# Turned B, x and sums behind later projections, a five-term log1p series, and products tied to the newest projection, in a Mamba-2 block on one core

## The chip, the cores and the metric

The kernel runs on 1 core of one Trainium2 chip (trn2). The metric is the device time of the whole kernel in microseconds (us); the number compared is the median over several runs. A core has five engines that work side by side: TensorE (PE, matmuls), VectorE (DVE), ScalarE (ACT), GpSimd (POOL) and SyncE (SP), which here issues the DMA transfers. Data lies in SBUF; matmuls write to PSUM.

## The reference

The input x has 4 rows of 512 tokens and 512 features. `c` gives, through a small product, six vectors for each row (shift, scale and gate of two branches).

```python
h = _layernorm(x) * (1 + ca) + sa
x = x + ga * attn(h)
h = _layernorm(x) * (1 + cb) + sb
x = x + gb * ffn(h)

# attn: Mamba-2 with chunks of 128 tokens
xBCzA = einsum('bld,ed->ble', h, in_proj_w)      # 2048 conv channels, 1024 z, 64 heads' A
xBC = silu(causal_conv4(xBCzA[..., :2048]) + conv_bias)   # x 1024, B 8 x 64, C 8 x 64
dt = softplus(A_log)                             # one per token and head
y = ssd_chunk_scan(x, -dt, B, C, 128) + D * x / dt
attn = einsum('bld,ed->ble', y * silu(z + z_bias), out_proj_w)
# ffn: a 512 x 512 product with weights binarized to sign * mean |w|
```

The scan has, for each chunk and head (64 heads of 16 features, 8 heads to a group), a product C·B of 128 x 128, times exp of differences of running sums of dt under a causal mask, times x; a state for each head that is carried from chunk to chunk; and C times that state.

## The kernel before, in words

**Tiling.** The tokens are cut into 8 halves h of 256 tokens, two to a row, and each half into 2 chunks c of 128. For each chunk the 8 groups go in 4 pairs gp; a (h, c, gp) is a unit, so there are 64 units, 8 in a half. One step handles one unit.

**The front of a half** turns tokens into the operands of its units. `load_x` and `f_norm` load and normalise. `f_hT` (L334) turns x with TensorE (tile phT) and writes hT with four ACT instructions (L346). `f_dt` (L352) multiplies hT with the A columns (pa, L367), and then runs a long chain, mostly on DVE, for softplus: u = exp(-|a|), then log1p(u) as the odd series 2 (w + w³/3 + …) in w = u / (u + 2). Its coefficients are SERIES (L36), one DVE scalar_tensor_tensor (STT) for each after the first (L379). After that come running sums of dt (L384), exps of them (L390 on), and the DMAs of sums, exps and D/dt to scratch in DRAM. `f_B`, `f_C`, `f_x` each make a pair of conv projections: `conv_pair` (L436) takes a PSUM tile (pp_), has `proj` (L431) issue four matmuls into it (L433), and reads it with one ACT instruction (L446) and three DVE STTs (L450); then tanh (L454) and a product (L455) for silu. `f_z` does the same without conv (uz, L512; thz, L516). `f_turned_sums` (L414) turns the sums with TensorE (pn) and copies them to st by ACT (L426); `f_Bt` (L476) turns B to tokens (pt_bt); `f_xt` (L485) turns x (pt_xt, L463), copies it with ACT into a padded tile xpad (L489), loads rr = D/dt on SP's queue (L498), and has POOL multiply (xs, L503).

**A unit** is made in three stages. `stage0` loads the running sums into a decay tile for each of the two groups r of the pair (`load_sums`, L537 and L538, two DMAs each on SP's queue). There are four such decay buffers, so a load waits until an earlier unit has done with the buffer. `stage1` multiplies the causal mask with C·B (gm, L619), runs `exps` (L545: 8 ACT instructions for each group, 16 a unit; bias from st) and multiplies both on DVE (L623). `stage2` makes py from decay and xpad, 16 small matmuls for each r, adds the contribution of the state and the skip term (L669 to L673), and updates the state from pst (L685). `burst` (L594) makes the products gy: C with the state for the current unit, C·B for a unit ahead. The tails of a chunk, `tail1` to `tail3`, are the output projection (po, L722), the second norm, its turn (ph, L740; h, L742) and the FFN product (pf, L758).

**Order of the work.** A scheduler of the framework orders the instructions within each engine from priorities and dependences, in the order in which the Python code issues them; engines wait for each other by semaphores. On top of it lie three means. Lists of steps, FIRST (half 0), SECOND (half 1) and FRONT (the later halves, L770), say in which step of the previous half's units a part of h's front is issued. `behind` (L764) puts a part after the last projection that was issued for that half (`tc.issue_after(H[h]["last"])`). `glued` (L208) issues the first of a group of small products (L211), and then the rest right after it with high priority (L214), so that the group stays together; it may take an instruction to come after. All PSUM tiles with the tag "mm" (projections, turns, pa, po, pf, pst, and so on) share five buffers, so each of them waits until the tile five before it has been read.

TensorE runs matmuls in four shapes of tiling: projections, turns, po and pf use all 128 rows and columns; gy has 64 rows, pa and pst 64 columns, py 32 columns.

Of the kernel before, what the change touches and what calls it, by code (L numbers as in the profile page):

```python
# [32 lines left out]

SERIES = [1.0 / k for k in range(17, 1, -2)]  # L36


@with_exitstack
def adaln_mamba_block(  # L40
# [18 lines left out]
    def bc(ap, n):  # L59

        return ap.unsqueeze(2).to_broadcast([ap.shape[0], ap.shape[1], n])
# [146 lines left out]
    def glued(products, after=None):  # L208

        with tc.issue_after(after) if after else nullcontext():  # L210
            first = products[0]()  # L211
        with tc.issue_after(first.ins), tc.high_priority(offset=1000):
            for product in products[1:]:
                product()  # L214
# [89 lines left out]
    H = [dict(B={}, C={}, xt={}, xs={}, bt={}, z={}) for _ in range(NHALF)]  # L304
# [47 lines left out]
    def f_dt(h):  # L352
# [23 lines left out]
        nc.vector.tensor_mul(q, u, u)  # L376
        nc.vector.tensor_scalar(dt, q, SERIES[0], None, ALU.mult)
        for cf in SERIES[1:]:
            nc.vector.scalar_tensor_tensor(dt, dt, cf, q, ALU.add, ALU.mult)  # L379
# [51 lines left out]
    def proj(pm, h, col, lo):  # L431
        for k in range(NK):
            last = mm(pm, win[:, k, col : col + P], H[h]["hT"][:, k, lo:], start=(k == 0), stop=(k == NK - 1))  # L433
        return last.ins

    def conv_pair(h, t0, name, dst=None):  # L436

        u = wk.tile([P, 2, T], F32, tag="u", name=f"u_{name}_{h}", bufs=4)
        for j in range(2):
            t = t0 + j
            pm = ps.tile([P, KS - 1 + T], F32, tag="mm", name=f"pp_{name}{j}_{h}")
            H[h]["last"] = proj(pm, h, t * P, 0)
            nc.scalar.activation(  # L446
                u[:, j, :], pm[:, KS - 1 :], AF.Identity, bias=cb[:, t : t + 1], scale=cw[:, t, KS - 1 : KS]
            )
            for k in range(KS - 1):
                nc.vector.scalar_tensor_tensor(  # L450
                    u[:, j, :], pm[:, k : k + T], cw[:, t, k : k + 1], u[:, j, :], ALU.mult, ALU.add
                )
        th = wk.tile([P, 2, T], F32, tag="th", name=f"th_{name}_{h}")
        nc.scalar.activation(th, u, AF.Tanh)  # L454
        nc.vector.scalar_tensor_tensor(u if dst is None else dst, th, 1.0, u, ALU.add, ALU.mult)  # L455
        return u
# [49 lines left out]
    def f_z(h, j):  # L506
        pm = ps.tile([P, 2, T], F32, tag="mm", name=f"pp_z{j}_{h}")
        for q in range(2):
            H[h]["last"] = proj(pm[:, q, :], h, NCONV + (2 * j + q) * P, KS - 1)
        u = wk.tile([P, 2, T], F32, tag="u", name=f"uz_{h}_{j}", bufs=4)  # L510
        for q in range(2):
            nc.scalar.activation(  # L512
                u[:, q, :], pm[:, q, :], AF.Identity, bias=zb[:, 2 * j + q : 2 * j + q + 1], scale=0.5
            )
        th = wk.tile([P, 2, T], F32, tag="th", name=f"thz_{h}_{j}")
        nc.scalar.activation(th, u, AF.Tanh)  # L516
        z = wk.tile([P, 2, T], F32, tag="z", name=f"z_{h}_{j}", bufs=6)
        nc.vector.scalar_tensor_tensor(z, th, 1.0, u, ALU.add, ALU.mult)
        H[h]["z"][j] = z
# [64 lines left out]
    def by_rows(gy, slot, h, c, gp, stationary):  # L584

        return [
            partial(
                mm, gy[:, r, slot, :], stationary[part],
                H[h]["C"][gp // 2][part, gp % 2, c * CH : (c + 1) * CH], start=True, stop=True,
            )  # L590
            for r, part in enumerate((slice(0, NS), slice(NS, P)))
        ]

    def burst(old, new):  # L594

        gy = ps.tile([P, 2, 4, CH], F32, tag="gy", bufs=1, name="gy_" + "_".join(map(str, old or new)))
        products = []
        if old is not None:
            h, c, gp = old
            k = (h % HPB) * 2 + c  # L600
            if k > 0:
                products += by_rows(gy, 1, h, c, gp, states[h // HPB, k][:, gp, :])
                G[old, 1] = gy
        if new is not None:
            h, c, gp = new
            products += by_rows(gy, 0, h, c, gp, H[h]["B"][gp // 2][:, gp % 2, c * CH : (c + 1) * CH])
            G[new, 0] = gy
        glued(products)

    def stage1(h, c, gp):  # L610

# [16 lines left out]
    def stage2(h, c, gp):  # L628

        n = f"{h}_{c}_{gp}"
        k = (h % HPB) * 2 + c
        b = h // HPB
        ets, e = U1.pop((h, c, gp))
        hd0 = c * NH + gp * HPP
        xp = H[h]["xt"][gp][:, c, :]
        xg = xp.rearrange("p (j q e) -> p j q e", q=4, e=HD)[:, :, 0:4:3, :]

        def by_head(v):

            return v.rearrange("p (j q) -> p j q", q=2).unsqueeze(3).to_broadcast([P, HPG, 2, HD])

        py = ps.tile([P, 2, CH], F32, tag="y", bufs=1, name=f"py_{n}")

        for r in range(2):
            glued([
                partial(
                    mm, py[32 * j : 32 * j + 32, r, :],  # L650
                    xp[:, r * 2 * P + 32 * (2 * j + q) : r * 2 * P + 32 * (2 * j + q) + 32],
                    ets[r][:, 2 * j + q, :], start=(q == 0), stop=(q == 1),
                )
                for q in range(2) for j in range(HPG // 2)
            ], H[1]["last"] if (h, c) == (0, 1) else None)

        cs = slice(c * CH, (c + 1) * CH)
        zg = H[h]["z"][gp][:, :, cs]
        xs = H[h]["xs"][gp][:, :, cs]
        t = wk.tile([P, 2, CH], F32, tag="gm", name=f"yt_{n}", bufs=3)  # L660

        ew = nc.vector if h == NHALF - 1 and c == 1 and gp >= NP // 2 else nc.gpsimd
        if k > 0:
            nc.vector.tensor_mul(t, G.pop(((h, c, gp), 1))[:, :, 1, :], e)
            if ew is nc.vector:
                ew.tensor_add(t, t, xs)
                ew.tensor_add(t, py, t)
            else:
                nc.vector.tensor_add(t, py, t)  # L669
                ew.tensor_add(t, t, xs)  # L670
        else:
            nc.vector.tensor_add(t, py, xs)  # L672
        ew.tensor_mul(zg, t, zg)  # L673

        if k < HPB * 2 - 1:
            if gp == 0:
                states[b, k + 1] = wk.tile([P, NP, P], F32, tag="S", name=f"S_{b}_{k + 1}")
            new = states[b, k + 1][:, gp, :]
            xd = wk.tile([P, HPG, 2, HD], F32, tag="xd", name=f"xd_{n}")
            nc.gpsimd.tensor_tensor(xd, xg, by_head(H[h]["ed"][:, hd0 : hd0 + HPP]), ALU.mult)  # L680
            xd2 = xd.rearrange("p j q e -> p (j q e)")
            pst = ps.tile([P, P], F32, tag="mm", name=f"pst_{n}")
            bt = H[h]["bt"][gp // 2][:, c, gp % 2, :]
            for r in range(2):
                mm(pst[r * NS : (r + 1) * NS, :], bt[:, r * NS : (r + 1) * NS], xd2[:, r * P : (r + 1) * P],  # L685
                   start=True, stop=True)
            if k == 0:
                nc.vector.tensor_copy(new, pst)
            else:
                nc.gpsimd.tensor_tensor(  # L690
                    new.rearrange("p (h e) -> p h e", e=HD),
                    states[b, k][:, gp, :].rearrange("p (h e) -> p h e", e=HD),
                    bc(H[h]["dec"][:, c * NP + gp, :], HD), ALU.mult,
                )
                nc.vector.tensor_add(new, new, pst)
# [68 lines left out]
    def behind(h, f, *args):  # L764
# [4 lines left out]

    FRONT = [  # L770
        (1, load_x, ()), (2, f_norm, ()), (3, f_hT, ()), (3, f_dt, ()),
        (4, f_B, (0,)), (4, f_C, (0,)), (5, f_x, (0,)), (5, f_x, (1,)), (5, behind, (f_turned_sums,)), (5, behind, (f_Bt, 0)),
        (6, f_B, (1,)), (6, behind, (f_xt, 0)), (6, f_C, (1,)), (6, behind, (f_xt, 1)),
        (7, f_x, (2,)), (7, behind, (f_Bt, 1)), (7, f_x, (3,)),
        (8, f_z, (0,)), (8, behind, (f_xt, 2)), (8, f_z, (1,)), (8, behind, (f_xt, 3)),
        (9, f_z, (2,)), (10, f_z, (3,)),
    ]

    FIRST = [
# [7 lines left out]

    SECOND = [
        (0, load_x, ()), (1, f_norm, ()), (2, f_hT, ()), (2, f_dt, ()), (2, f_B, (0,)), (3, f_C, (0,)), (3, f_x, (0,)),
        (4, f_x, (1,)), (4, behind, (f_turned_sums,)), (4, behind, (f_Bt, 0)),  # L790
        (5, f_B, (1,)), (5, behind, (f_xt, 0)),
    ]
    SECOND += FRONT[FRONT.index((6, f_C, (1,))) :]
    NU = 2 * NP
# [28 lines left out]
    h = NHALF - 1  # L823
# [65 lines left out]
```

## Time and profile before

| what | us |
|---|---|
| median of three runs | 749.24 (748.86 to 753.6) |
| the profiled execution | 747.6 |
| span in its profile, first to last instruction | 745.9 |
| PE busy | 711.2 (5196 matmuls) |
| weight loads busy | 503.2 |
| DVE busy | 602.6 (1218 instructions) |
| ACT busy | 523.7 (1507) |
| POOL busy | 260.4 (313) |

The profile is of one execution, so its 747.6 stands beside the median of 749.24; the 1.7 between the execution and its span lie before the first and after the last instruction. The mean clock that TensorE was granted is 0.991 of full speed. A view of waits lists which engine sat idle before which work, and what released it; a timeline gives each instruction or run of equal instructions with its start, its duration and, in brackets, the idle time ahead of it. "PE pp_x L433" is TensorE working on tile pp_x at line 433. The work of the halves repeats: the stretches from 184 to 271, 271 to 361, 361 to 447.5, 447.5 to 536.5 and 536.5 to 623 us each hold one half, with PE busy 85.75 of 87.0, 87.29 of 90.0, 85.25 of 86.5, 87.27 of 89.0 and 85.25 of 86.5.

### The profile page before, as it was taken

What the parts mean: (1) busy time and instruction counts of PE and PEld (TensorE: products, weight loads), DVE (VectorE), ACT (ScalarE), POOL (GpSimd) and SP (SyncE); (2) the same over time, 40 slices, a digit from 0 to 9 for tenths busy, and PEclk for the clock granted to TensorE, in tenths of its full rate; (3) what the DMA queues carried; (4) which work ended last, traced back from release to release, by engine and by line L of the source; (5) the groups of instructions that cost most, each with busy time, mean ns of one, the idle gap of its engine ahead of it and who ended that gap; (6) DMA issues with size and microseconds to landing.
All of it is one profiled execution on the core that took longest, in us unless ns stands there. A gap on an engine that the chain in (4) does not pass through costs nothing.

```text
span 745.9 us, 15107 instructions
## 1 busy us (share of the span) xinstructions
PE 711.2 (95%) x5196; PEld 503.2 (67%) x5196; DVE 602.6 (81%) x1218; ACT 523.7 (70%) x1507; POOL 260.4 (35%) x313
## 2 busy tenths in 40 slices
PE   6999979899999999999999999999999999999997
PEld 3787647566677666686667666876667866677654
DVE  3968889866999579986899769996699867997795
ACT  2476668648796596775877777764969658798941
POOL 4021325334242433353224243533324232343452
PEclk9999989899999999999999999999999999999999
DMA  8991865435654266434634246543544436458610
GB/s 280 317 289 39 237 164 121 113 86 138 125 146 125 63 158 140 106 101 99 158 101 119 75 108 165 149 110 69 139 125 121 129 79 175 104 152 167 143 58 28
DMA packets 119068, 99.25 MB, mean 133 GB/s; under 512 B 73984, under 2 KB 97152, under 8 KB 118992
## 3 DMA queue, kind: packets, MB, share of 16 engines
q1 hardware_dynamic: 117808, 96.39, 50.6%
q0 software_dynamic: 896, 1.38, 0.6%
q8 instruction: 41, 0.67, 0.4%
q10 hardware_dynamic: 288, 0.52, 0.2%
q14 instruction: 35, 0.29, 0.1%
HBM read 92.47 MB, written 5.79 MB: 132 GB/s over the span
## 4 chain that ended last, share of the span: by engine, by line
PE 77%; ACT 14%; DVE 5%; issue 2%; DMA 2%; ACTq 0%; POOL 0%; SPq 0%; DVEq 0%
PE pp_x L433 16%; PE po L722 15%; PE pp_z L433 12%; ACT decay L545 10%; PE pp_B L433 7%; PE pp_C L433 7%; PE pf L758 4%; PE py L211 3%; PE py L214 3%; PE gy L211 2%; PE pt_xt L463 2%; PE pst L685 2%; PE pa L367 1%; DMA decay<-sums_d 1%; ACT h L742 1%
## 5 line engine op out<-in xcount | busy, mean ns | idle before, releaser
L545 ACT ACTIVATE decay<-decay,st 128x128 f32<-128x128 f32 x960 | 293.0, 395 | 4.0 <-DMA decay<-sums_d 3.7
L623 DVE SCALAR_TENSOR_TENSOR decay<-decay,gm 128x1024 f32<-128x1024 f32 x120 | 156.8, 1308 | 25.1 <-ACT decay L545 24.1
L433 PE MATMUL pp_x<-hT,win 128*128 128x259 f32 x512 | 122.5, 394 | 5.8 <-ACT decay L545 5.8
L433 PE MATMUL pp_z<-hT,win 128*128 128x256 f32 x512 | 118.1, 383 | 0.0
L433 PEld LDWEIGHTS pp_x<-hT,win 128*128 128x128 f32 x512 | 98.0, 195 | 24.1 <-ACT decay L545 6.0
L722 PE MATMUL po<-wout,z 128*128 128x512 f32 x256 | 113.9, 595 | 0.0
L433 PEld LDWEIGHTS pp_z<-hT,win 128*128 128x128 f32 x512 | 94.3, 189 | 16.1 <-issue 3.3
L680 POOL TENSOR_TENSOR xd<-xpad,st 128x256 f32<-128x256 f32 x48 | 37.6, 784 | 188.3 <-PE pst L685 143.0
L450 DVE SCALAR_TENSOR_TENSOR u_x<-pp_x,cw,u_x 128x256 f32<-128x256 f32 x192 | 82.9, 473 | 1.4 <-ACT u_x L446 0.5
L722 PEld LDWEIGHTS po<-wout,z 128*128 128x128 f32 x256 | 47.4, 190 | 52.6 <-issue 51.7
L512 ACT ACTIVATE uz<-pp_z,zb 128x256 f32<-128x256 f32 x64 | 26.8, 468 | 62.3 <-PE pp_z L433 62.3
L670 POOL TENSOR_TENSOR yt<-yt,xs 128x256 f32<-128x256 f32 x46 | 41.1, 893 | 84.4 <-DVE yt L669 84.4
L214 PE MATMUL py<-decay,xpad 128*32 128x128 f32 x1680 | 67.4, 276 | 0.0
L673 POOL TENSOR_TENSOR z<-yt,z 128x256 f32<-128x256 f32 x62 | 58.5, 944 | 17.1 <-DVE yt L672 13.6
L433 PE MATMUL pp_B<-hT,win 128*128 128x259 f32 x256 | 60.9, 388 | 0.9 <-ACT st L426 0.9
L758 PE MATMUL pf<-bwT,h 128*128 128x512 f32 (+1 forms) x136 | 59.1, 575 | 0.8 <-ACT h L742 0.6
L433 PE MATMUL pp_C<-hT,win 128*128 128x259 f32 x256 | 59.0, 382 | 0.0
L503 POOL TENSOR_TENSOR xs<-u_x,rr 128x512 f32<-128x512 f32 x32 | 42.1, 1318 | 40.8 <-DVE u_x L455 40.8
L433 PEld LDWEIGHTS pp_B<-hT,win 128*128 128x128 f32 x256 | 47.0, 189 | 10.8 <-ACT st L426 1.7
L433 PEld LDWEIGHTS pp_C<-hT,win 128*128 128x128 f32 x256 | 47.8, 189 | 7.8 <-DVE u_B L450 0.3
L446 ACT ACTIVATE u_x<-pp_x,cb,cw 128x256 f32<-128x256 f32 x64 | 35.2, 559 | 25.1 <-PE pp_x L433 24.8
L211 PE MATMUL py<-decay,xpad 128*32 128x128 f32 x240 | 47.5, 280 | 3.8 <-ACT decay L545 2.8
(155 smaller groups left out, 1134.0 us busy)
## 6 DMA issues: line engine op xcount, KB each, us to landing
decay<-sums_d SPq DMA_DIRECT2D x120, 256.0 KB
decay<-sums_d SPq DMA_DIRECT2D x120, 128.0 KB
rr<-r_d SPq DMA_DIRECT2D x64, 128.0 KB
e<-e_d SPq DMA_DIRECT2D x96, 64.0 KB
win<-in_w_inT SPq DMA_DIRECT2D x4, 1024.0 KB
xr<-in_x SPq DMA_DIRECT2D x16, 256.0 KB
res<-o SPq DMA_DIRECT2D x15, 256.0 KB
x<-in_x SPq DMA_DIRECT2D x14, 256.0 KB
```

Of the source, the lines that this page charges most:

```text
L211: first = products[0]()
L214: product()
L433: last = mm(pm, win[:, k, col : col + P], H[h]["hT"][:, k, lo:], start=(k == 0), stop=(k == NK - 1))
L450: nc.vector.scalar_tensor_tensor(u[:, j, :], pm[:, k : k + T], cw[:, t, k : k + 1], u[:, j, :], ALU.mult, ALU.add)
L503: nc.gpsimd.tensor_tensor(xs, xc, rr, ALU.mult)
L545: nc.scalar.activation(ets[r][:, i, :], ets[r][:, i, :], AF.Exp, bias=H[h]["st"][:, hd : hd + 1], scale=-1.0)
L623: nc.vector.scalar_tensor_tensor(ets[r], ets[r], 1.0, bc_mid(gm[:, r, :], HPG), ALU.min, ALU.mult)
L670: ew.tensor_add(t, t, xs)
L673: ew.tensor_mul(zg, t, zg)
L680: nc.gpsimd.tensor_tensor(xd, xg, by_head(H[h]["ed"][:, hd0 : hd0 + HPP]), ALU.mult)
L722: last_po = mm(po, H[h]["z"][g // 2][:, g % 2, c * CH : (c + 1) * CH], wout[:, g, :], start=(g == 0), stop=(g == NKI - 1))
L758: mm(pf, h2[:, k, :], bwT[:, k, cols], start=(k == 0), stop=(k == NK - 1))
```

## The change

SERIES has five coefficients in place of eight, fitted to the range instead of 1/17 to 1/3. `proj` records its last matmul in `newest["proj"]`; `burst` ties its products to the newest projection, and stage2 ties py to it for every unit (before only for the units of half 0's second chunk, to `H[1]["last"]`). The step lists put the turns of sums, of B and of x later: sums from behind x1 to behind B1, xt_0 from behind B1 to behind C1, xt_1 from behind C1 to behind x2, Bt_0 from behind x1 to behind x2, Bt_1 from behind x2 to behind z0, xt_2 from behind z0 to behind z1, xt_3 from behind z1 to behind z2. SECOND loses its own entries for Bt_0 and xt_0, since those now come with the part of FRONT that it takes over; its sums stay where they were, in step 4 behind x1. FIRST is unchanged.

```diff
-SERIES = [1.0 / k for k in range(17, 1, -2)]
+SERIES = [0.11612164612, 0.108532879004, 0.142961789972, 0.19999853166, 0.333333336603]
...
             last = mm(pm, win[:, k, col : col + P], H[h]["hT"][:, k, lo:], start=(k == 0), stop=(k == NK - 1))
+        newest["proj"] = last.ins
         return last.ins
+
+    newest = {}
...
-        glued(products)
+        glued(products, newest["proj"])
...
                 for q in range(2) for j in range(HPG // 2)
-            ], H[1]["last"] if (h, c) == (0, 1) else None)
+            ], newest["proj"])
...
     FRONT = [
         (1, load_x, ()), (2, f_norm, ()), (3, f_hT, ()), (3, f_dt, ()),
-        (4, f_B, (0,)), (4, f_C, (0,)), (5, f_x, (0,)), (5, f_x, (1,)), (5, behind, (f_turned_sums,)), (5, behind, (f_Bt, 0)),
-        (6, f_B, (1,)), (6, behind, (f_xt, 0)), (6, f_C, (1,)), (6, behind, (f_xt, 1)),
-        (7, f_x, (2,)), (7, behind, (f_Bt, 1)), (7, f_x, (3,)),
-        (8, f_z, (0,)), (8, behind, (f_xt, 2)), (8, f_z, (1,)), (8, behind, (f_xt, 3)),
-        (9, f_z, (2,)), (10, f_z, (3,)),
+        (4, f_B, (0,)), (4, f_C, (0,)), (5, f_x, (0,)), (5, f_x, (1,)),
+        (6, f_B, (1,)), (6, behind, (f_turned_sums,)), (6, f_C, (1,)), (6, behind, (f_xt, 0)),
+        (7, f_x, (2,)), (7, behind, (f_xt, 1)), (7, behind, (f_Bt, 0)), (7, f_x, (3,)),
+        (8, f_z, (0,)), (8, behind, (f_Bt, 1)), (8, f_z, (1,)), (8, behind, (f_xt, 2)),
+        (9, f_z, (2,)), (9, behind, (f_xt, 3)), (10, f_z, (3,)),
     ]
...
-        (4, f_x, (1,)), (4, behind, (f_turned_sums,)), (4, behind, (f_Bt, 0)),
-        (5, f_B, (1,)), (5, behind, (f_xt, 0)),
+        (4, f_x, (1,)), (4, behind, (f_turned_sums,)),
+        (5, f_B, (1,)),
     ]
```

## The prediction

> **What bounds the kernel now.** I read the page's busy times first, then the view of waits for PE, then PE's and ACT's timelines where those waits lie.
>
> ```profile
> span 745.9 us, 15107 instructions
> ...
> PE 711.2 (95%) x5196; PEld 503.2 (67%) x5196; DVE 602.6 (81%) x1218; ACT 523.7 (70%) x1507; POOL 260.4 (35%) x313
> ...
> PEclk9999989899999999999999999999999999999999
> ```
>
> TensorE is busy 711.2 of 745.9 us and the change neither adds nor removes a matmul. So only the 34.7 us of PE idle, and the few matmuls run at a reduced clock, can move. PEclk dips in two of the 40 slices, the 6th (93 to 112 us) and the 8th (131 to 149), nowhere else.
>
> ```profile
> PE pp_x L433 <- ACT decay L545: 5.8, 1, 5.8
> PE pa L367 <- ACT hT L346: 3.8, 4, 1.2
> PE pst L685 <- ACT xpad L489: 3.2, 1, 3.2
> PE py L211 <- ACT decay L545: 2.8, 3, 0.9
> PE pt_xt L463 <- DVE u_x L455: 1.5, 1, 1.5
> ```
>
> Columns: total us, times, longest. (A 6.0 us wait of pg before the first projection is not touched.) The big ones are single waits in the first two halves; `pa` and `py` wait once in every half. Their surroundings in PE's timeline (start, duration, work, idle before):
>
> ```profile
> 92.09 0.44 PE L685 MATMUL pst<-xd,bt 128*64 128x128 f32 x4
> 98.30 5.44 PE L433 MATMUL pp_x<-hT,win 128*128 128x259 f32 x16 [5.77 <-ACT decay L545]
> ```
>
> ```profile
> 133.62 0.69 PE L685 MATMUL pst<-xd,bt 128*64 128x128 f32 x4 [3.20 <-ACT xpad L489]
> 134.24 6.25 PE L433 MATMUL pp_x<-hT,win 128*128 128x259 f32 x16
> ```
>
> Sixteen projection passes take 3.51 us elsewhere. After the two long idles they take 5.44 and 6.25, so each idle costs itself plus 1.9 or 2.7 us.
>
> In the steady halves the ACT queue decides what PE waits for. ACT idles 8.20 us before its uz at 433.66, then is dense up to hT, on which `pa` and all later projections depend:
>
> ```profile
> 433.66 0.84 ACT L512 ACTIVATE uz<-pp_z,zb 128x256 f32<-128x256 f32 x2 [8.20 <-PE pp_z L433]
> 434.39 2.44 ACT L545 ACTIVATE decay<-decay,st 128x128 f32<-128x128 f32 x8
> ...
> 443.30 0.83 ACT L512 ACTIVATE uz<-pp_z,zb 128x256 f32<-128x256 f32 x2
> 444.01 2.45 ACT L545 ACTIVATE decay<-decay,st 128x128 f32<-128x128 f32 x8
> 446.35 0.64 ACT L516 ACTIVATE thz<-uz 128x512 f32<-128x512 f32 x1
> 446.87 1.93 ACT L346 ACTIVATE hT<-phT,modT 128x256 f32<-128x256 f32 x4
> 448.69 2.45 ACT L545 ACTIVATE decay<-decay,st 128x128 f32<-128x128 f32 x8
> ```
>
> [...] idles of 5.77 and 3.20 us were followed by slow projections, those of 1.2 us were not. [...] The trace: 3.51 us for 16 passes after full-tile work, 3.70 to 3.77 after py or pst, so about 0.2 per switch.
>
> **The change part by part.** I compared the order of instructions on each engine in both programs, and what each waits for.
>
> *Series.* Three of seven STTs at L379 go, in 8 f_dt: 24 instructions at 0.28 us busy, 0.20 us start to start, so 0.6 us of DVE latency per half, 4.8 in all. In steady halves the dt chain has several projections (3.51 us a pair) to hide in, so it costs nothing there; without that cover it would be 0.6 a half. It counts only in the first half and at 75 to 100.
>
> *First half.* gy of (0,0,0) moves behind z0 and pt_xt_1; DVE is 0.6 us earlier. The wait of pt_xt (1.48, until 34.06) shrinks: bounds 0.6 and 1.2 plus, **-1.0**.
>
> *75 to 100 us, half 1's first projections.* Before, gy and py of (0,0,2) filled the time in which ACT makes hT, with a wait of 1.07 in the middle, and pa ended at 80.26. Now pa and pp_B precede them, pa ends near 78.2, and the dt chain starts 2 us sooner and is 0.6 shorter. The pp_x that waited till 98.30 actually needs a PSUM buffer that DVE frees after u_C (L450), queued behind the dt chain. In the new order pp_x of the first pair waits for a DVE copy of states near 90.1 (PE idle about 2.2), and the next pair for u_C0 near 95 (idle about 0.9). 5.77 + 1.07 becomes 3.1 to 3.6: **-3.3** (bounds -1.5 and -4). Clock: neither new idle reaches 3.2, but they are close together; of 1.9 I take **-1.0**, bounds 0 and -1.9.
>
> *120 to 140.* With xt_0 behind C1 instead of B1, pst no longer sits behind xpad; it waits for u_C1 (near 131.6), then pp_x for xpad0 (132.6), and 0.7 us of gy moved after pf. **-0.9**, clock **-1.3** of 2.7, bounds 0 and -2.7.
>
> *Even boundaries (halves 2, 4, 6).* At 359.2 PE has finished phT and idles 1.17 until hT, then does pa interleaved with py and gy. Now gy (0.65) and py's first row (0.6) come before pa and cover it: -1.1 x 3 = **-3.4**. If they find their own wait (gm, decay), it is nothing.
>
> *Odd boundaries (3, 5, 7): a loss.* py of (c=0, gp=2)'s first row now precedes pf instead of following it, 2.3 us earlier (441.1 against 443.4). That frees the decay buffer, so SP issues the loads of the next chunk's first unit sooner, and the schedule places that unit's exps ahead of hT on ACT. Before, four groups of 8 exps stand between uz and the end of hT; now six do, plus one xpad copy (0.46). From 433.2: uz 0.72, group 2.35, thz 0.52, xpad 0.46, group 2.35, h 1.43, two groups 4.70, uz 0.72, group 2.35 with thz 0.52, hT 0.48, group 2.35, hT 1.43: 20.4, so hT ends at 453.6 instead of 448.7, 4.9 later. Queued behind hT are pa, the dt chain and every projection. Other PE work moved ahead of it: py's two rows, gy and pst. PE then runs pp_B k by k as hT's quarters land; after the last at 453.6 remain pa's last products and about 2.4 us of pp_B, so the pair ends near 456.4 instead of 453.6: +2.7 x 3 = **+8.1**. Bounds: 0 (if ACT gets through its queue early in its 8 us idle, which the order forbids for uz but not if z comes sooner) and 4.9 x 3 = +14.7 (no cover).
>
> *Turned B, x, sums one or more projections later.* Eleven small waits (0.16 to 0.85 us: pt_xt, pt_bt, pp_B on st, ph on st) sum to 3.5 us over the run. The turns' inputs now have 3.5 us more: **-3.0**, bounds 0 and -3.5. What is late next: xpad, then xd on POOL and pst; POOL is 35% busy. No transfer is moved by this but rr's, on an SP queue that is mostly idle.
>
> *Products behind the newest projection.* PE's mode switches fall from 312 to 304: 8 x 0.17 = **-1.4**. The tail after 690 keeps its order: 0.
>
> Sum: -1.0 -3.3 -1.0 -0.9 -1.3 -3.4 -3.0 -1.4 +8.1 = -7.2. Span 745.9 - 7.2 = 738.7, profiled execution 747.6 - 7.2 = 740.4. The median of the three runs (749.24, from 748.86 to 753.6) is 1.6 above the profiled one, so the median becomes 742.0, 1.0% less.
>
> **The rivals.**
> A. *No odd loss.* The exps ahead of hT are absorbed. For it: ACT idles 8.2 us before uz; against: those exps stand behind uz[...]. Then -15.3, and with the rest of the clock's loss back (0.9 and 1.4) -17.6: 731.6 to 733.9.
> B. *Startup waits only change names.* For it: pp_x waits for DVE anyway, and DVE is 90% busy in 75 to 100 (22.41 of 25). Then 75 to 140 gives nothing: -7.2 + 6.5 = -0.7, 748.5.
> C. *Slower.* The odd loss decides: above 2.7 + 7.2 / 3 = 5.1 us each the sign flips. hT 4.9 us late without cover, and then a half-clock pair at 2.7 us, is 7.6 each, 14.7 more than I have: -7.2 + 14.7 = +7.5, 756.7. With cover but the half clock, -7.2 + 8.1 = +0.9, 750.1. For it: idle of some 3.6 us within 9; against: it is broken by py, gy and pa.
> D. *The change does not do what it says:* products tied to a projection would already stand there. Then only the series is left, 0.6 in the first half and 0.6 to 0.9 at 75 to 100, about -1.5: 747.7. The new order speaks against it.
>
> **How the numbers follow.** My forecast (738 to 746) 0.42, A 0.27, B and D 0.16, C 0.15. A measurement of this kernel tells about 1% from no change: faster by over 1% is below 741.7, which takes A and a good half of my own case: 0.50; slower by over 1% is above 756.7, only the far end of C: 0.05; the rest 0.45. For eight in ten I go from A's middle, 732.5, to 751.0, C's covered form. The likeliest case alone has 738 to 746.
>
> **What would show it.** Right: pa's waits at even boundaries gone; three waits of pa or pp_B for hT of together 2 to 4 us near 360 + 90 x n, with two groups of exps just ahead of hT in ACT's timeline; no wait over 3.2 us after 70; PEclk nearer full in slices 6 and 8. Wrong: pp_x still waits 5 us near 95, or odd boundaries with hT no later than before (A), or with slow projections after them (C).

## The result, and the profile after

The changed kernel is slower: 755.38 us (median of 20 runs, 752.23 to 759.6) against 748.83 for the kernel before on the same chips; the ratio of after to before is 1.0088, with a 95% interval of 1.0069 to 1.0108. The profiled execution took 753.95, with a span of 752.2. That is 6.35 above the profiled execution of before. I had forecast 742.0, with a range up to 751.0.

The page of the kernel after, the same lines as before the change:

```profile
span 752.2 us, 15128 instructions
...
PE 714.1 (95%) x5196; PEld 502.8 (67%) x5196; DVE 597.9 (79%) x1194; ACT 522.1 (69%) x1507; POOL 259.4 (34%) x313
...
PEclk9999999999999999999999999999999999999999
```

DVE lost its 24 instructions, TensorE did the same 5196 passes. The view of waits for PE, after (total us, times, longest):

```profile
PE pp_B L434 <- DVE u_x L454: 5.9, 6, 1.4
PE py L212 <- DVE decay L627: 4.4, 3, 1.5
PE pst L689 <- DVE u_C L454: 3.2, 1, 3.2
PE gy L212 <- DVE gm L623: 2.6, 4, 1.2
PE pa L368 <- ACT hT L347: 2.3, 6, 1.1
PE pp_x L434 <- DVE S L692: 2.2, 1, 2.2
PE ph L744 <- DVE t L300: 1.8, 2, 1.3
PE pf L762 <- DVE u_B L454: 1.7, 3, 0.6
```

The 5.8 us wait of pp_x is now 2.2 and 0.6, and those of pa for hT are shorter. In their place stand waits for DVE, in nearly every half: u_x, the masked decay, gm, u_B. PE's idle time rose from 34.7 to 38.1 us.

Where the time went is best seen from the start of the same matmul in both traces. Cut at the first matmul of z3 and of C0 of each half, the span after minus before is:

| stretch | forecast | measured |
|---|---|---|
| up to z3 of half 0 | -1.0 | -0.06 |
| to z3 of half 1 (75 to 140 us lie here) | -6.5 | -4.17 |
| z3 to C0 over the boundaries to halves 2, 4, 6 | -3.4 | -2.41 |
| z3 to C0 over the boundaries to 3, 5, 7 | +8.1 | +9.52 |
| C0 to z3 inside halves 2 to 7 | -3.0 | +2.78 |
| after z3 of half 7 | 0 | +0.70 |
| mode switches, over all | -1.4 | (in the above) |
| sum | -7.2 | +6.4 |

The inner stretches are +3.28 in halves 2, 4, 6 and -0.50 in 3, 5, 7. Adjacent stretches trade with each other, so only differences of several us between kernels are read below.

The odd boundary looks as I had worked it out. ACT's timeline after, in front of half 5:

```profile
439.41 4.79 ACT L549 ACTIVATE decay<-decay,st 128x128 f32<-128x128 f32 x16
444.08 0.83 ACT L516 ACTIVATE uz<-pp_z,zb 128x256 f32<-128x256 f32 x2
444.79 0.41 ACT L549 ACTIVATE decay<-decay,st 128x128 f32<-128x128 f32 x1
445.09 0.64 ACT L520 ACTIVATE thz<-uz 128x512 f32<-128x512 f32 x1
445.61 2.16 ACT L549 ACTIVATE decay<-decay,st 128x128 f32<-128x128 f32 x7
447.65 0.57 ACT L347 ACTIVATE hT<-phT,modT 128x256 f32<-128x256 f32 x1
448.10 2.46 ACT L549 ACTIVATE decay<-decay,st 128x128 f32<-128x128 f32 x8
450.44 1.48 ACT L347 ACTIVATE hT<-phT,modT 128x256 f32<-128x256 f32 x3
```

Two groups of eight exps stand among and ahead of hT. hT is done at 451.9; z3 of half 4 began 1.6 us earlier than before, so against it hT is 4.7 us later than before (448.8), where I had 4.9. PE's timeline after shows what that does at the same place, and what I had missed:

```profile
446.49 0.30 PE L212 MATMUL py<-decay,xpad 128*32 128x128 f32 x1 [1.46 <-DVE decay L627]
...
447.62 0.37 PE L212 MATMUL gy<-C,B 64*128 64x128 f32 x1 [0.49 <-DVE gm L623]
...
448.27 0.44 PE L368 MATMUL pa<-hT,win 128*64 128x128 f32 x4 [0.16 <-ACT hT L347]
```

The cover that was moved ahead of pa has waits of its own (1.46 for the masked decay, 0.49 for gm). They come to 1.95, more than twice the 0.92 that py waited here before.

### The profile page after: what moved, and what is told of

It reads as the page before. It is cut to its first block, busy times and chain, and to the rows that moved or that the text cites. A ratio compares the mean times of both kernels' runs of the same rounds, so it can differ in the third digit from the quotient of the medians.

```text
span 752.2 us, 15128 instructions
## 1 busy us (share of the span) xinstructions
PE 714.1 (95%) x5196; PEld 502.8 (67%) x5196; DVE 597.9 (79%) x1194; ACT 522.1 (69%) x1507; POOL 259.4 (34%) x313
## 4 chain that ended last, share of the span: by engine, by line
PE 63%; ACT 18%; DVE 11%; DMA 4%; issue 3%; POOL 1%; SPq 0%; ACTq 0%; DVEq 0%
PE po L726 12%; PE pp_x L434 11%; ACT decay L549 11%; PE pp_z L434 11%; PE pp_B L434 6%; PE pp_C L434 4%; PE pf L762 4%; DMA decay<-sums_d 3%; DVE decay L627 3%; PE py L215 2%; PE py L212 2%; PE gy L212 2%; ACT win L549 2%; PE pa L368 1%; DVE u_x L454 1%
## 5 line engine op out<-in xcount | busy, mean ns | idle before, releaser
L684 POOL TENSOR_TENSOR xd<-xpad,st 128x256 f32<-128x256 f32 x48 | 41.1, 856 | 178.0 <-PE pst L689 131.6
L434 PE MATMUL pp_B<-hT,win 128*128 128x259 f32 x256 | 65.6, 401 | 6.3 <-DVE u_x L454 5.9
L507 POOL TENSOR_TENSOR xs<-u_x,rr 128x512 f32<-128x512 f32 x32 | 44.3, 1384 | 49.0 <-DVE u_x L459 46.6
```

Source lines behind the costliest of these rows:

```text
L507: nc.gpsimd.tensor_tensor(xs, xc, rr, ALU.mult)
```

## The experiments

Ratios are to the kernel before on the same chip, with 95% intervals. Tables of stretches are made as above, from one profiled execution of each kernel against that of before; it can lie a few us off the median.

**1. One of the moves put back: xt_3.**

```diff
-        (8, f_z, (1,)), (8, behind, (f_xt, 2)),
-        (9, f_z, (2,)), (9, behind, (f_xt, 3)), (10, f_z, (3,)),
+        (8, f_z, (1,)), (8, behind, (f_xt, 2)), (8, behind, (f_xt, 3)),
+        (9, f_z, (2,)), (10, f_z, (3,)),
```

> The changed kernel with one edit: the turn of x's last quarter (xt_3) stands behind z1 again, in step 8, as before the change. Theory (ACT order at the odd boundaries): in this order no group of exps of the next unit stands ahead of hT any more, so the losses of 2.9 to 3.4 us in front of halves 3, 5 and 7 go, 9.5 in all, two of four half-clock stretches with them: the median falls from 755.4 to about 746, ratio to before about 0.996. Rival (the small matmuls tied to projections cost, whatever ACT does): the boundary keeps its cost, 754 to 756, ratio 1.007 to 1.01.

Measured: 741.77, ratio 0.9902 (0.987 to 0.9933). More than the 9.5 I had expected: 1.9% of the time hangs on this one turn, and without its move the change is a gain of 1%. In this kernel's table the odd boundaries are at 0.00, and the inner stretches at -1.72 (halves 2, 4, 6) and -1.04, together -2.8. The even boundaries are at -0.08: their gain of 2.4 hung on the same move. The waits for u_x, u_B and the masked decay are gone from its view of waits for PE:

```profile
PE pa L368 <- ACT hT L347: 4.9, 5, 1.2
...
PE py L212 <- ACT decay L549: 2.8, 3, 0.9
...
PE pp_B L434 <- ACT h L746: 1.9, 3, 0.9
```

**2. The sums put back** behind x1 (step 5), all else as changed.

> The changed kernel with one edit: the turned sums stand behind x1 in step 5 again. Theory (PSUM buffers): with pn no longer between x1 and B1, pp_B of B1 takes a buffer that three DVE instructions of u_x have to free; put back, the waits of pp_B for u_x (0.70 in even, 1.1 to 1.4 us in odd halves, 5.9 in all) shrink to what they were before the change (0.3 for st): about -4, 751.5, ratio 1.004. Rival (pn itself then waits as long for the same buffer): no change, 755, ratio 1.008.

Measured: 755.33, ratio 1.0094 (1.0062 to 1.0126). My theory fell. In even halves it is now ph that waits about 1.1 us for u_x: what is late there is DVE's u_x, whichever tile comes next. In odd halves pp_B now waits for st (1.0 to 1.9).

**3. The moves alone** (FRONT and SECOND; eight terms, old ties).

> The kernel before with only the step lists of the change (FRONT and SECOND), eight terms and the old ties. Theory (the moves carry both the loss at odd boundaries and the mid-half waits): about as slow as the full change, without the 2 to 4 us that the earlier pa in half 1 and the shorter series gave: 756 to 760, ratio 1.010 to 1.015. Rival (the ties of products to the newest projection make the loss): close to before, 747 to 750.

Measured: 756.63, ratio 1.0116 (1.0082 to 1.0151), as the theory has it. The ties do not make the loss.

**4. The series alone.**

```diff
-SERIES = [1.0 / k for k in range(17, 1, -2)]
+SERIES = [0.11612164612, 0.108532879004, 0.142961789972, 0.19999853166, 0.333333336603]
```

> The kernel before with only the five-term series. Theory: 24 short DVE instructions are off the path in steady halves; only the first two halves can gain: -0.5 to -1.5, 747.3 to 748.3, ratio 0.998 to 0.999. Rival (the dt chain holds u_C and its PSUM buffers in half 1, and DVE is full there): up to -4, 745, ratio 0.994.

Measured: 746.27, ratio 0.998 (0.997 to 0.9989): -1.5, the theory's far end, and what I had for rival D of the prediction.

**5. xt_3 alone moved late**, in the kernel before.

> The kernel before with one edit: the turn of x's last quarter (xt_3) stands behind z2 (step 9) instead of behind z1 (step 8). Theory (this one move makes the loss: it lets the exps of the next chunk's first unit stand ahead of hT on ACT): the 13.9 us by which putting it back helped the changed kernel appear here as a loss, 758 to 763, ratio 1.014 to 1.02. Rival (it hurts only together with the other moves): 747 to 751, ratio 0.998 to 1.004.

Measured: 756.04, ratio 1.0118 (1.0076 to 1.016). One move of a 0.6 us turn by one projection pair costs 1.2%. It falls short of the 758 to 763 expected; in the full change it costs more, 1.9%. Its table has the marks of the changed kernel: -2.35 at the even boundaries and +3.05 inside the even halves, +14.79 at the odd boundaries, of which 8.37 come back inside the odd halves.

**6. hT first**, with xt_3 still late.

```diff
-        (1, load_x, ()), (2, f_norm, ()), (3, f_hT, ()), (3, f_dt, ()),
+        (1, load_x, ()), (2, f_norm, ()), (2, f_hT, ()), (3, f_dt, ()),
```

> The changed kernel with one edit: f_hT stands in step 2 of the list instead of step 3, so that hT is issued before the next unit's exps; xt_3 stays behind z2. On ACT the two groups of exps come after hT again. Theory (the place of these exps in ACT's queue is the cost, not xt_3's turn itself): the losses at odd boundaries go, and what follows from them: 742 to 747, ratio 0.992 to 0.998. Rival (the later turn delays xpad, py and the state by itself): 752 to 756, ratio 1.005 to 1.01.

Measured: 752.31, ratio 1.0065 (1.005 to 1.008), inside the rival's numbers; the interval overlaps with that of the changed kernel. ACT's timeline has hT ahead of the two groups again, and the odd boundaries fell from +9.52 to +3.08. But the inner stretches of the even halves rose from +3.28 to +6.10. The view of waits for PE of this kernel:

```profile
PE pa L368 <- ACT hT L347: 6.6, 8, 1.4
...
PE pp_B L434 <- ACT h L746: 4.5, 3, 1.6
...
PE pf L762 <- DVE u_B L454: 2.9, 3, 1.0
```

So the place of the exps makes most of the boundary's loss, but not the loss of the kernel: in these traces PE gives back nearly all that it gains there, by waiting for ACT and DVE elsewhere (the spans are 752.1 and 752.2).

**7. xt_3 put back, ties taken out.**

> The changed kernel with xt_3 behind z1 again and without the ties of gy and py to the newest projection. Theory (ties only reorder small products inside stretches where PE is busy anyway, and help once, where pa comes earlier in half 1): 743 to 746, ratio 0.993 to 0.997. Rival (the moves and the series bring all the gain): 741 to 742.5, ratio 0.99.

Measured: 745.66, ratio 0.997 (0.9958 to 0.9983). The ties are worth 0.7%, and its table says where: the stretch to z3 of half 1 is +1.44 here and -2.46 with them; the other stretches agree within 0.5.

**8. xt_3 put back and hT first.**

> The changed kernel with xt_3 behind z1 again and f_hT in step 2. If the waits of pa for hT (1.17 us in halves 2, 4, 6) and of py (0.92 in 3, 5, 7) come from hT's place behind other work on ACT and PE, they shrink: up to 6.3 us less than 741.8, so 736 to 740, ratio 0.983 to 0.989. If hT waits for the turn phT on PE, nothing is gained: 741 to 743, ratio 0.99.

Measured: 743.52, ratio 0.9939 (0.9918 to 0.996), its interval overlapping with 0.9902's. No gain from pulling hT ahead could be seen.

**9. The turn late, the skip term early.** f_xt cut in two; turn and xpad copy behind z2, rr loads and xs behind z1.

> The changed kernel with f_xt of x's last quarter cut in two: the turn and ACT's copy to xpad stay behind z2, while the loads of rr and POOL's product xs stand behind z1 again. Theory (the place of the turn and its copy in PE's and ACT's queues makes the loss): nothing is won, 753 to 757, ratio 1.007 to 1.012. Rival (the later rr loads and xs delay POOL and the product z): most of the 13.9 us comes back, 742 to 746, ratio 0.992 to 0.998.

Measured: 753.93, ratio 1.0085 (1.0043 to 1.0127), as the changed kernel. But this run tests little: its trace has the same order of instructions as the changed kernel up to the last half. The rr loads and xs had not become late there. The last xs starts 17.3 to 17.7 us ahead of z3 in halves 3 to 5 after the change, and 15.8 to 18.2 ahead of it before. So it is the trace of the changed kernel, and not this run, that speaks against POOL and the transfers, and leaves the turn and its copy.

**10. Eight terms in the changed kernel.**

> The changed kernel with the eight-term series of before, so that every dt chain on DVE is 0.6 us longer. Theory (in the middle of the halves PE now waits for u_x and u_B on a DVE that is late): the 0.6 us come through at the waits of most halves, +2.5 to +5, 758 to 760, ratio 1.012 to 1.015. Rival (the chain is covered as before the change, where three terms were worth 1.5 us): +0.5 to +1.5, 756 to 757, ratio 1.009 to 1.011.

Measured: 767.28, ratio 1.022 (1.0171 to 1.027): 1.3% for 0.6 us of DVE in each half, far above both. The trace of this kernel, the slowest of its four runs, has ten half-clock stretches (granted clock 0.50) of 3.4 us or more between its first and its last matmuls, against four in the changed kernel: 41.0 us against 13.7. If a busy us at a granted clock of 0.50 does half a us of work (an estimate; by it the 16 passes at 98.30 and 134.24 us before, which took 5.44 and 6.25 us with 3.46 and 5.07 of them at 0.50, both come to 3.71, where undisturbed ones took 3.62 to 3.87), 13.1 of the 16.0 us between the two spans are the clock's, and PE's idle time is only 2.8 us longer.

**11. Bt_1, xt_2 and xt_3 put back.**

> The changed kernel with Bt_1 behind x2, xt_2 behind z0 and xt_3 behind z1, as before the change; sums, xt_0, xt_1 and Bt_0 stay late. If xt_3 alone carried the loss and Bt_1's and xt_2's later places are harmless or help: 741.5 to 744, ratio 0.991 to 0.995. If two turns behind z1 crowd ACT there: 738 to 741, ratio 0.986 to 0.990.

Measured: 742.79, ratio 0.9924 (0.9901 to 0.9948). Bt_1's and xt_2's later places do nothing that can be told from experiment 1.

**12. xt_3 put back, gy's tie alone.**

> The changed kernel with xt_3 behind z1 again and only burst's gy tied to the newest projection, py as before. The two ties together were worth 3.9 us there (745.7 without, 741.8 with). Theory (pa in half 1 comes earlier because gy of (0,0,2), with the py behind it, moves after it): gy's tie carries it, 741.5 to 743, ratio 0.991 to 0.993. Rival (py's tie carries it): 744.5 to 746, ratio 0.995 to 0.998.

Measured: 741.76, ratio 0.9909 (0.9882 to 0.9937). All that the ties bring comes from gy's. The tie of py brings nothing that could be seen.

**13. xt_3 put back, eight terms.**

> The changed kernel with xt_3 behind z1 again and the eight-term series: the control for the run of eight terms with xt_3 late, where three terms cost about 10 us. Theory (DVE is late only because xt_3's move made it lose time in front of the half): here the three terms cost what they cost the kernel before, 1 to 2.5 us, 743 to 745, ratio 0.992 to 0.996. Rival (with the ties and the other moves, DVE bounds the stretch from hT to the middle of the half anyway): 748 to 752, ratio 1.0 to 1.005.

Measured: 750.83, ratio 1.0029 (1.0008 to 1.0051), the rival's numbers. But not by the rival's way: compared with experiment 1 the same matmuls start 1.14 us later at z3 of half 0, 5.7 later at z3 of half 1, and then 5.6 to 6.6 later at C0 and z3 of every half. So 4.6 of 6.3 us arise in half 1, and 0.7 in the six halves after it. There, with xt_3 early, DVE's 0.6 us are covered. In experiment 10, with xt_3 late, the same three terms cost another 6.7 us after z3 of half 1, but not by waits: PE's idle time there is 20.9 us, against 21.0 in the changed kernel, and its half clock 20.5 against 6.8. (The medians of experiments 13 and 1 lie 1.3% apart, some 9.5 us; their traces show 6.3 of it.)

**14. Two terms in the changed kernel** (a coarser log1p).

> The changed kernel with only the last two of the five coefficients, so that log1p is a coarser approximation and the dt chain on DVE is 0.6 us shorter. Theory (PE waits for a late DVE in the middle of the halves, 0.70 and 0.53 us in even ones): 0.4 to 1 us less in each half, 3 to 6 in all and perhaps half-clock stretches with them, 748 to 752, ratio 1.0 to 1.005. Rival (the order in front of odd halves sets the time, whatever DVE does): 754 to 756, ratio 1.007 to 1.01.

Measured: 752.71, ratio 1.0051 (1.0022 to 1.0081): -0.4% against the changed kernel, just past the weak end of the theory and hardly clear of noise. The even inner stretches went from +3.28 to -0.72, the odd ones from -0.50 to +3.59: in these traces a shorter DVE chain removes the waits in one half and as much comes back in the next.

The best kernels were experiments 1 and 12, 0.9 to 1.0% faster than before and 1.8 to 1.9% faster than the changed one.

## Why the prediction was wrong, point by point

**The odd boundaries: right in kind, 9.5 for 8.1.** The two groups of exps stood ahead of hT, and in experiment 6, with hT first, this stretch lost 6.4 us less, though the kernel as a whole won little. Its cause was named one link short: I had it from py's first row in front of pf and the decay loads behind it. Experiments 1 and 5 show that xt_3's later turn brings this whole order about: around hT, ACT has the order of the changed kernel in experiment 5 and that of before in experiment 1; whether it does so through py and the loads was not tried alone. I also counted gy and py as cover at no cost: they waited 1.95 us themselves.

**The middle of the halves: the step that failed.** "The turns' inputs now have 3.5 us more: -3.0", with xpad and then POOL named as late next and charged nothing. Measured: +2.8. The small waits that I had counted went, but PE now waits 5.9 us for DVE's u_x and 1.7 for its u_B. What was late next was DVE, which I had at nothing in these halves. With xt_3 early the same step gives -2.8 (experiment 1), so the size was right for all turns but one. For xt_3 I looked at what its turn waits for, and not at how the order of the other engines changes with it.

DVE's order is where the waits are seen. Directly ahead of the STT that ends each of the nine waits for u_x and u_B (0.53 to 1.42 us) stands a masked decay, which takes 1.2 to 2.2 us. In the even halves of experiment 1 it stands behind that STT. Half 4 after the change, where PE's pp_B waits 0.70 us until 387.11, for the fifth STT of u_x:

```profile
382.92 0.95 DVE L300 TENSOR_SCALAR t<-xr,mv_f,rs_f 128x512 f32<-128x512 f32 x1 [1.05 <-POOL rs_f L298]
383.79 1.65 DVE L454 SCALAR_TENSOR_TENSOR u_x<-pp_x,cw,u_x 128x256 f32<-128x256 f32 x4
385.36 1.21 DVE L627 SCALAR_TENSOR_TENSOR decay<-decay,gm 128x1024 f32<-128x1024 f32 x1
386.49 1.65 DVE L454 SCALAR_TENSOR_TENSOR u_x<-pp_x,cw,u_x 128x256 f32<-128x256 f32 x4
```

The same place in experiment 1, where five STTs are done before the decay and PE does not wait:

```profile
379.02 0.47 DVE L454 SCALAR_TENSOR_TENSOR u_x<-pp_x,cw,u_x 128x256 f32<-128x256 f32 x1
380.88 0.55 DVE L300 TENSOR_SCALAR t<-xr,mv_f,rs_f 128x512 f32<-128x512 f32 x1 [1.39 <-POOL rs_f L298]
381.35 1.65 DVE L454 SCALAR_TENSOR_TENSOR u_x<-pp_x,cw,u_x 128x256 f32<-128x256 f32 x4
...
383.52 1.21 DVE L627 SCALAR_TENSOR_TENSOR decay<-decay,gm 128x1024 f32<-128x1024 f32 x1
```

DVE's pauses tell the two kernels apart less: in 48 us of half 4 those of over 0.25 us sum to 5.3 us after the change and to 5.0 in experiment 1, though most of the 5.3 are for exps and none of the 5.0. That xt_3's move makes these waits is shown by experiment 1; alone, in experiment 5, the move brings other waits of PE for DVE (5.4 us for the masked decay, 3.0 for gm, 1.5 for u_B). That it does so through the place of the decay is read from the traces and was not tried by itself. Experiments 6 and 14 show the other side: what is won at one place comes back as a wait for ACT or DVE at another.

**The series: mis-sized by what depends on it.** Alone it gives -1.5, as I had. "In steady halves it costs nothing" held for the waits (0.7 us in six halves in experiment 13, no more idle time in experiment 10), but with xt_3 late the half clock that came with the three terms cost nearly 7 us there, by the same estimate. In half 1, together with the ties and moves, three terms are worth 4.6 us (experiments 1 and 13), for 0.6 of DVE time; about 1.6 of it is the clock's. I added effects that were not additive.

**Half 1: -4.2 for -6.5.** The wait of pp_x for a copy of states came as worked out (2.18 for 2.2, at 90.9 for 90.1). The wait of 3.20 in front of pst did not shrink; only what releases it changed, from xpad to u_C. In this stretch PE's idle time fell by 2.9 us for the 4.2 forecast; the rest of the -4.2 is the clock's, as worked out next.

**The clock: its price was missing.** I took one idle of 3.2 us as the limit, and charged no half clock at the odd boundaries in my own case, because py, gy and pa would break the idle time there. Before, two stretches of 6.83 us ran at a granted clock of 0.50; after, four of 3.41, two in half 1 as before and two new ones in front of halves 3 and 7. The sum is the same, but before PE was idle in 4.5 us of it anyway, and after in 0.15. Half of the busy rest is lost, by the estimate of experiment 10: 4.6 us before, 6.7 after. So half 1 won about 1.2 of the 2.3 us forecast, and the odd boundaries lost about 3.4.

**Even boundaries: -2.4 for -3.4, and given back.** pa's waits of 1.17 us went, as forecast (pa had them in front of halves 2, 4 and 6 alone, and py its 0.92 in front of 3, 5 and 7). But it is xt_3's move that did it: experiment 5 has this gain without the ties, experiment 1 the ties without it. PE's idle time at these boundaries fell from 3.5 to 0.4 us and rose inside the same halves from 1.0 to 4.0. So of this gain little was left at the end of the half.

**The start (0 for -1.0) and the mode switches (-1.4).** Of the 0.86 us won at z0 about 0.6 were lost again by C1, behind gy's new place. Mode switches, counted in the traces, fall from 315 to 312, not by 8. Their price of 0.2 us came from two different measures: 3.51 is from the first pass to the start of the next work, 3.70 to 3.77 from the first start to the last end. With either one measure the difference before is about 0.1 us (after full-tile work 3.51 against 3.61 after py, or 3.67 against 3.77), so this term was worth some 0.3 us.

**Rivals.** Against A I had that the exps stand behind uz on ACT; that they could not pass it was my assumption. After the change they stood behind it again: ACT idled 8.49 us until uz at 431.64, and the next exps ran from 432.37. C had the sign, and one of its means, the half clock, came in front of two of the three odd halves. But it needed 5.1 us at each odd boundary, and 3.2 was measured. The slower time came from the gains that failed: 15.3 us forecast, 3.2 measured. The range ended at 751, because B and C were thought of one at a time.

## What to carry to other kernels

When a small step is moved on the busiest engine, read off the order of the other engines what now stands ahead of the next stage's first input there, and price that: here a 0.6 us turn, moved by one projection pair, cost 14 us. With PE at 95% and DVE at 81%, gains were not additive here; what PE won at one place was kept only as far as DVE and ACT kept up until the next place where PE waits for them. Try each move of a package alone, whether the package is a gain or a loss. And look in the trace whether an edit changed the order that it was to change: in experiment 9 it hardly did.

## What the runs showed of the hardware

TensorE's half clock needs less idle time than I thought. The grants in the traces change on a grid of 3.41 us: before at 94.93, 101.76, 132.48 and 139.31 us, after at 91.70, 95.12, 129.25, 132.66, 269.20, 272.61, 627.60 and 631.01, in each trace whole multiples of 3.41 apart. Over the sixteen profiled kernels here (after the first 20 us, counting windows at full clock): of 40 windows in which PE was idle for 1.9 us or more, all were followed by half clock; with 1.55 to 1.9 us, 10 of 17; with 1.0 to 1.55, none of some 110. In the traces of before and after alone it is all of 6 with 1.9 or more, and none of 13 with 1.0 to 1.55. So 1.9 us in a window, somewhat over half of it, was always enough here, in one piece (2.07 us from 130.41 on, before) or in several (1.45, 0.49 and 0.21 us at 265.8, after). The wait of 3.20 us before the change, shorter than such a window, was a first sign. The changed kernel in windows on this grid (length, then PE busy; PEclk is the third number from the right):

```profile
265.79:269.20 3.41, 1.26 (x26) 0.72 (x22) 3.15 (x6) 3.41 (x12) 1.19 (x3) 1.00 0.66 200
269.20:272.61 3.41, 3.41 (x16) 2.09 (x16) 2.75 (x4) 3.41 (x11) 1.37 (x3) 0.50 0.91 274
...
443.26:446.67 3.41, 1.95 (x36) 1.42 (x36) 3.41 (x5) 3.41 (x12) 1.76 (x2) 1.00 0.69 156
446.67:450.08 3.41, 2.29 (x31) 1.25 (x23) 3.06 (x7) 3.41 (x12) 2.12 (x3) 1.00 0.99 342
```

The same waits occur in front of halves 3 and 5. At 265.8 they fall into one window (2.15 us idle) and the next runs at 0.50; at 443 the grid cuts them in two (1.46 and 1.12), and the window after each runs at 1.00. Where the grid falls differs from trace to trace: between before and after by 0.19 us, counted from the start of the span. Among the 20 runs of the changed kernel those with a lower mean clock tend to be slower (752.23 us at 0.995, 759.6 at 0.983, but also 759.52 at 0.989); that the place of the grid makes this spread is likely, and not shown.
